# Turning the second half's x: TensorE transposes against 32x32 squares and VectorE transposes

## The chip, the cores and the metric

The kernel runs on one core of a Trainium2 chip. The time is device microseconds of one execution. A profile shows one execution in detail: the instructions of TensorE (PE for matmuls, PEld for weight loads), VectorE (DVE), ScalarE (ACT) and GpSimd (POOL), and the queue of SyncE (SP), which issues nearly all transfers between HBM and the on-chip memory SBUF. Matmul results land in PSUM, in banks of 128 partitions by 512 f32.

## The reference: gated experts and a residual

For x of 8 batches, 512 positions and 256 features, each of 8 experts and one shared expert computes a gated layer with 1024 hidden columns, and the results are added to x with weights per batch:

```
g = h @ Wg[e];  u = h @ Wu[e]                  # 256 -> 1024
expert[e] = (silu(g) * u) @ Wd[e]              # 1024 -> 256
mixed = sum_e gates[b, e] * expert[e]          # 8 experts
shared = (silu(h @ Sg) * (h @ Su)) @ Sd
out = x + (1 - s[b]) * mixed + s[b] * shared   # h is x
```

## The kernel before

**Algorithm and passes.** The batches are taken in two passes (`h` = 0 and 1) of `NI` = 4 batches each. In a pass the 4 batches are combined with 4 column groups of the weights by a scheme of sums and differences with the points `CI` = 0, 1, -1, 2, so that fewer products are needed. A unit is one pass, one expert and one half of the hidden columns: 2 x 9 x 2 = 36 units, run one after another. The first half of a unit's work is `gate_up` (P, Q, R1 and R steps, L404 to L469), the second is `down` (L501 to L606), which runs interleaved with the next unit's `gate_up`.

**How x gets its layout.** The matmuls contract over features, so x must lie with the features on the partitions: `[128 features, 2 halves, 512 positions]`. `load_rows` (L147) brings a batch in as rows, position `4p + t` on partition p. TensorE transposes against an identity matrix turn it, four 128x128 blocks into one PSUM bank (`turn`, L143), and ScalarE or VectorE copies the bank to SBUF. VectorE also forms x0 - c*x1 there, for the batches with c not zero.

For the first pass `turn_x` (L157) does this at the very start. For the second pass `prepare(1)` (L178) does it as background work. It is a Python generator, and the main loop takes one step of it (L836) at every fifth step of `down` from the third unit on. For each of the four batches it loads the rows into buffers of `iopool` (4 buffers of 128x512 f32), lets two steps pass, turns and copies half 1 (L191 to L196), then half 0, and stores both in `xd` in HBM (L200). Afterwards, for each of six pairs of batches, it loads `f` tiles back from `xd` (L208), lets GpSimd form sums and differences, and stores them in `xs`. The second pass loads `v` and `b` from there; the first pass has written its own `xs` from what the first unit forms with VectorE and GpSimd (L238, L240, L252, L253).

**PSUM banks of `down`.** `new_po` (L134) deals out two banks, po0 and po1. A turn takes the next bank without moving the counter (`turns=True`) and sets `turned`. `seeded` (L524) normally copies an accumulator into the bank with ScalarE (L530), lets the matmul add to it, and copies it back (L539); after a turn in that bank it does a plain matmul, and `put` (L505) adds the result to the accumulator on VectorE (L518).

**What sets the order.** `HAND` (L770) names TensorE and GpSimd: their instructions run in the order of the program text. ScalarE does so in the first unit alone. The order of VectorE, of ScalarE later on and of SP is chosen by a scheduler when the kernel is built: it places an instruction as soon as its inputs and buffers are there by its own estimate. On the chip each queue then runs strictly in that order.[...]

Of the kernel before, what the change touches and what calls it, by code (L numbers as in the profile page):

```python
# [11 lines left out]
ALU = mybir.AluOpType  # L12
# [4 lines left out]
def kernel(  # L17
# [37 lines left out]
    nc = tc.nc  # L55
    B, S, D = x.shape
    E, _, F = Wg.shape
    P = 128
    NT = S // P
    NE = E + 1  # L60
    NI = 4
    GRP = F // (NI * P)
    NH = B // NI
    CI = (0.0, 1.0, -1.0, 2.0)
# [22 lines left out]
    iopool = ctx.enter_context(tc.tile_pool(name="io", bufs=4))  # L87
# [10 lines left out]
    ve = nc.vector  # L98
# [31 lines left out]
    turned = [False, False]  # L130
# [3 lines left out]
    def new_po(name, turns=False):  # L134

        k = po_next[0]
        if held[k]:
            k = 1 - k
        if not turns:
            po_next[0] = 1 - k  # L140
        return ps_o.tile([P, S], F32, tag=f"po{k}", name=name), k

    def turn(bank, blocks):  # L143
        for t, block in enumerate(blocks):
            nc.tensor.transpose(bank[:, ts(t, P)], block, ident)

    def load_rows(pool, tag, b):  # L147
        rows = []
        for c in range(2):
            t = pool.tile([P, 2, D], F32, tag=tag, name=f"xin{b}_{c}")  # L150
            nc.sync.dma_start(
                t, x[b].rearrange("(p t) d -> p t d", t=NT)[:, 2 * c : 2 * c + 2, :]
            )
            rows.append(t)
        return rows

    def turn_x(h, rows):  # L157

        for i in range(NI):
            xt = xpool.tile([P, 2, S], F32, tag="x", name=f"x{h}_{i}")  # L160
            for n_, k in enumerate((0, 1) if CI[i] == 0.0 else (1, 0)):
                pt, n = new_po(f"ptx{h}_{i}_{k}")
                turn(pt, [rows[i][t // 2][:, t % 2, ts(k, P)] for t in range(NT)])
                turned[n] = True
                if k == 1:
                    nc.scalar.copy(xt[:, 1], pt)
                elif CI[i] == 0.0:
                    ve.tensor_copy(xt[:, 0], pt)  # L168
                else:
                    ve.scalar_tensor_tensor(  # L170
                        xt[:, 0], xt[:, 1], -CI[i], pt, ALU.mult, ALU.add
                    )
                if n_ == 1:
                    xhub[h, i] = xt
                yield

    def prepare(h):

        def tile_of(name):
            return iopool.tile([P, S], F32, tag="io", name=f"{name}{h}")  # L180

        for i in range(NI):
            to = xdram[h, i] = dram.tile([P, 2, S], F32, tag=f"xd{h}_{i}", name=f"xd{h}_{i}")
            rows = load_rows(iopool, "io", NI * h + i)
            yield
            yield
            both = {}
            for k in (1, 0):
                pt, n = new_po(f"ptx{h}_{i}_{k}", True)
                turned[n] = True  # L190
                turn(pt, [rows[t // 2][:, t % 2, ts(k, P)] for t in range(NT)])  # L191
                both[k] = tile_of(f"xt{i}_{k}_")
                if k == 1 or CI[i] == 0.0:
                    nc.scalar.copy(both[k], pt)
                else:
                    ve.scalar_tensor_tensor(both[0], both[1], -CI[i], pt, ALU.mult, ALU.add)  # L196
                yield
            yield
            for k in (1, 0):
                nc.sync.dma_start(to[:, k], both[k])  # L200
            yield
        for p, (i, j) in enumerate(PAIRS):
            d = CI[i] - CI[j]
            to = dram.tile([P, 3, S], F32, tag=f"xs{h}_{p}", name=f"xs{h}_{p}")
            at = []
            for n, k in ((i, 0), (j, 0), (j, 1), (i, 1)):
                t = tile_of(f"f{p}_{n}_{k}_")
                nc.sync.dma_start(t, xdram[h, n][:, k])  # L208
                at.append(t)
            yield  # L210
            yield
            v = at[0]
            gp.tensor_tensor(v, v, at[1], ALU.subtract)
            if d != 1.0:
                gp.tensor_scalar(v, v, 1.0 / d, 0.0, ALU.mult, ALU.add)
            yield
            gp.tensor_tensor(at[2], v, at[2], ALU.add)
            yield
            gp.tensor_tensor(at[3], v, at[3], ALU.add)
            yield  # L220
            yield
            yield
            for k, n in ((0, 0), (1, 2), (2, 3)):
                nc.sync.dma_start(to[:, k], at[n])
            scratch[h, p] = to
            yield
# [551 lines left out]
    for i in range(NI):  # L778
        loaded.append(load_rows(hpool, "h", i))
        load_w(units[0], i)  # L780
    turning = turn_x(0, loaded)
    for _ in range(2):
        next(turning)
# [4 lines left out]
    for i in range(NI):  # L788
        make_at(units[0], i)
    behind, acc, ahead = iter(()), {}, prepare(1)  # L790
    for u in units:
        final = u.closes
# [5 lines left out]
        for what in FIRST if u.n == 0 else LAST if nxt is None else ORDER:  # L798
# [27 lines left out]
            elif what == "X":  # L826
                i, j, pools = TAILS.pop(0)
# [59 lines left out]
```

## Time and profile before

| | |
|---|---|
| median of 3 runs | 2461.21 us (2460.86 to 2461.64) |
| the profiled execution | 2461.27 us |
| its span in the profile | 2459.3 us |
| turns of the second pass (L145, tile xin, 100 to 450 us) | 32 matmuls of 128x128, from 178.8 us on |
| ScalarE copies and VectorE forms after them (L194, L196) | 5 and 3, between 180 and 431 us |
| stores of xd (L200) | 8, between 180.5 and 431.1 us |
| VectorE busy, 20 to 40 us and 40 to 60 us | 19.93 and 17.69 of 20 us |
| GpSimd busy, 20 to 40 us and 40 to 60 us | 19.30 and 19.36 of 20 us |

The profile page first gives each engine's busy time, then the chain of work that ended last, followed back from the end. A timeline row gives start and length in microseconds, engine, line, operation, output and inputs; a bracket at the end gives the idle time before it and who ended it. Matmuls are pipelined and their ends modelled, so the distance of starts tells more than their lengths.

### The profile page before, as it was taken

To read this page: it belongs to the slowest core of one execution; us is meant where nothing else is said; L and a number is where in the kernel's file an instruction comes from. 1 tells how busy PE (TensorE), PEld (TensorE's weight loads), DVE (VectorE), ACT (ScalarE), POOL (GpSimd) and SP (SyncE) were. 2 spreads that over 40 slices of the span, in tenths; PEclk is the share of its full clock that TensorE was granted. 3 is DMA by queue.
4 is the path that set the end of the run, shared out by engine and by line. 5 is a ranking of instruction groups with operands and counts; after the bars stand their busy time and mean duration, and the time that the engine had idled before them with its cause. 6 is when DMAs were issued, how large, how long until landed. Compare 5 with 4: busy or idle time off the path is not lost.

```text
span 2459.3 us, 22816 instructions
## 1 busy us (share of the span) xinstructions
PE 2440.4 (99%) x5782; PEld 1084.0 (44%) x5782; DVE 1931.9 (79%) x2876; ACT 1246.4 (51%) x2305; POOL 2092.8 (85%) x2335
## 2 busy tenths in 40 slices
PE   9999999999999999999999999999999999999998
PEld 4444444444444444444444444444444444444444
DVE  7777787787777777777987777778777777777787
ACT  4555445545555555455455555555555555555543
POOL 7988888898898998888878888888888888888883
PEclk9999999999999999999999999999999999999999
DMA  5333333443333333333443233223333333223332
GB/s 168 95 93 103 97 113 107 124 132 107 109 115 94 119 97 106 110 116 113 127 144 94 88 90 98 86 86 99 99 103 103 94 103 90 86 89 96 91 93 82
DMA packets 180801, 255.83 MB, mean 104 GB/s; under 512 B 14016, under 2 KB 114368, under 8 KB 180672
## 3 DMA queue, kind: packets, MB, share of 16 engines
q1 hardware_dynamic: 180384, 254.33, 34.1%
q8 instruction: 49, 0.80, 0.1%
q14 instruction: 80, 0.66, 0.1%
q10 hardware_dynamic: 288, 0.04, 0.0%
HBM read 238.59 MB, written 15.73 MB: 103 GB/s over the span
## 4 chain that ended last, share of the span: by engine, by line
PE 89%; POOL 6%; DVE 2%; issue 1%; ACT 0%; DMA 0%; DVEq 0%; POOLq 0%; ACTq 0%
PE c L461 28%; PE c L451 14%; PE c L429 9%; PE c L407 9%; PE r L547 7%; PE r L570 7%; PE S L531 5%; PE b L531 5%; PE q L547 5%; PE s L547 2%; POOL cols L488 2%; POOL rows L488 1%; POOL wb L345 0%; DVE h L398 0%; POOL wb L346 0%
## 5 line engine op out<-in xcount | busy, mean ns | idle before, releaser
L461 PE MATMUL c<-b,wb 128*128 128x512 f32 x1728 | 847.3, 592 | 0.0
L393 ACT ACTIVATE sg<-c 128x512 f32<-128x512 f32 x576 | 343.6, 597 | 590.0 <-DVE c L466 336.9
L398 DVE SCALAR_TENSOR_TENSOR h<-sg,coef,c 128x512 f32<-128x512 f32 x576 | 428.1, 743 | 247.5 <-PE c L461 139.8
L461 PEld LDWEIGHTS c<-b,wb 128*128 128x128 f32 x1728 | 327.8, 190 | 410.0 <-issue 388.7
L451 PE MATMUL c<-v,u 128*128 128x512 f32 x864 | 441.7, 593 | 0.4 <-ACT c L446 0.3
L488 POOL TENSOR_TENSOR rows<-rows,h 128x512 f32<-128x512 f32 x282 | 371.1, 1316 | 0.0
L456 DVE TENSOR_TENSOR c<-D,c 128x512 f32<-128x512 f32 x432 | 299.1, 693 | 78.5 <-ACT sg L393 58.5
L488 POOL TENSOR_TENSOR cols<-cols,h 128x512 f32<-128x512 f32 x282 | 359.9, 1276 | 0.0
L466 DVE TENSOR_TENSOR c<-c,D 128x512 f32<-128x512 f32 x432 | 298.8, 692 | 20.1 <-PE c L461 19.9
L345 POOL TENSOR_TENSOR wb<-u,wb 128x256 f32<-128x256 f32 x108 | 79.0, 732 | 237.3 <-ACT wb L343 237.3
L407 PE MATMUL c<-x,w 128*128 128x512 f32 x576 | 277.9, 595 | 0.3 <-DVE x L168 0.3
L451 PEld LDWEIGHTS c<-v,u 128*128 128x128 f32 x864 | 162.9, 190 | 205.9 <-issue 165.3
L547 PE MATMUL r<-h,wd 128*128 128x512 f32 x426 | 217.7, 592 | 0.2 <-DVE xt L196 0.2
L570 PE MATMUL r<-X,ud 128*128 128x512 f32 x426 | 217.6, 592 | 0.0
L477 DVE TENSOR_TENSOR X<-h,h 128x512 f32<-128x512 f32 x213 | 210.4, 988 | 6.9
L429 PE MATMUL c<-x,at 128*128 128x512 f32 x432 | 209.6, 593 | 2.5 <-DVE P L422 2.2
L439 ACT COPY D<-c 128x512 f32<-128x512 f32 x284 | 165.9, 584 | 87.2 <-DVE h L398 87.2
L488 POOL TENSOR_TENSOR rows<-h,h 128x512 f32<-128x512 f32 x144 | 198.4, 1378 | 0.0
L488 POOL TENSOR_TENSOR cols<-h,h 128x512 f32<-128x512 f32 x144 | 184.2, 1279 | 0.0
L412 ACT COPY P<-c 128x512 f32<-128x512 f32 x216 | 126.6, 586 | 111.4 <-PE c L407 107.0
L407 PEld LDWEIGHTS c<-x,w 128*128 128x128 f32 x576 | 109.1, 191 | 135.0 <-issue 112.1
L530 ACT COPY S<-accS 128x512 f32<-128x512 f32 x134 | 79.1, 590 | 150.4 <-DVE accV L518 142.6
(105 smaller groups left out, 3482.4 us busy)
## 6 DMA issues: line engine op xcount, KB each, us to landing
b<-xs SPq DMA_DIRECT2D x210, 512.0 KB, 3.6
v<-xs SPq DMA_DIRECT2D x210, 256.0 KB, 2.6
w<-in_L_cond_Wg_dram SPq DMA_DIRECT2D x128, 128.0 KB, 3.5
w<-in_L_cond_Wu_dram SPq DMA_DIRECT2D x128, 128.0 KB, 3.6
wd<-in_L_cond_Wd_dram SPq DMA_DIRECT2D x32, 512.0 KB, 4.9
xin<-in_x_dram SPq DMA_DIRECT2D x24, 256.0 KB, 3.4
f<-xd SPq DMA_DIRECT2D x24, 256.0 KB, 3.2
xs<-f SPq DMA_DIRECT2D x18, 256.0 KB, 2.0
```

Of the source, the lines that this page charges most:

```text
L393: nc.scalar.activation(s, bank, AF.Silu)
L398: ve.scalar_tensor_tensor(t, u.sg[i, j], coef[:, u.e, b : b + 1], bank, ALU.mult, ALU.mult)
L407: nc.tensor.matmul(bank, u.raw[i][:, m, 0], xhub[u.h, i][:, 0], start=True, stop=True)
L429: nc.tensor.matmul(bank, u.at[i][:, m], xhub[u.h, i][:, 1], start=False, stop=True, skip_group_check=True,)
L451: nc.tensor.matmul(bank, u.U[p][:, m], u.V[p], start=False, stop=True, skip_group_check=True)
L456: ve.tensor_sub(other, u.Ds[j, m], bank)
L461: nc.tensor.matmul(bank, u.W[p][:, r, m], u.VB[p][:, r], start=False, stop=True, skip_group_check=True,)
L466: ve.tensor_add(bank, bank, u.Ds[j, m])
L488: gp.tensor_tensor(sums[n], u.h_[n, n] if first else sums[n], u.h_[at], ALU.add)
L531: nc.tensor.matmul(po, w, b, start=not full, stop=True, skip_group_check=full)
L547: nc.tensor.matmul(po, w, b, start=True, stop=True)
L570: nc.tensor.matmul(A, u.Ud[p], u.X[p], start=False, stop=True, skip_group_check=True)
```

## The change

In `prepare`, each half of a batch is loaded by four transfers (`load_turned`) instead of the whole batch by two. Transfer q brings 32 features of the half to partitions 32q to 32q+31. On the way the positions are arranged so that every 32x32 square of the tile holds 32 positions by 32 features, in pieces of 32 f32, 128 bytes. One VectorE transpose of 128x512 turns every square in place of the four TensorE transposes and writes SBUF directly. For half 0 of the batches with c not zero a VectorE instruction then forms xt0 - c*xt1 from SBUF. The column order of the result differs from before only in how it comes about: column t*128 + p still is position 4p + t. The first pass's `turn_x` stays as it was.

```diff
+    def load_turned(to, b, k):
+        at = x[b].rearrange("(c r t) d -> r t c d", r=32, t=NT)
+        for q in range(4):
+            nc.sync.dma_start(
+                to[ts(q, 32)].rearrange("r (t c d) -> r t c d", t=NT, d=32),
+                at[:, :, :, ts(4 * k + q, 32)],
+            )
+
@@ prepare
-            rows = load_rows(iopool, "io", NI * h + i)
+            rows = [tile_of(f"xin{i}_{k}_") for k in range(2)]
+            for k in (1, 0):
+                load_turned(rows[k], NI * h + i, k)
             yield
             yield
             both = {}
             for k in (1, 0):
-                pt, n = new_po(f"ptx{h}_{i}_{k}", True)
-                turned[n] = True
-                turn(pt, [rows[t // 2][:, t % 2, ts(k, P)] for t in range(NT)])
                 both[k] = tile_of(f"xt{i}_{k}_")
-                if k == 1 or CI[i] == 0.0:
-                    nc.scalar.copy(both[k], pt)
-                else:
-                    ve.scalar_tensor_tensor(both[0], both[1], -CI[i], pt, ALU.mult, ALU.add)
+                ve.transpose(both[k], rows[k])
+                if k == 0 and CI[i] != 0.0:
+                    ve.scalar_tensor_tensor(
+                        both[0], both[1], -CI[i], both[0], ALU.mult, ALU.add
+                    )
                 yield
```

## The prediction

> **What bounds the kernel now.** I read the page first: engine sums, then the chain that ended last.
>
> ```profile
> span 2459.3 us, 22816 instructions
> PE 2440.4 (99%) x5782; PEld 1084.0 (44%) x5782; DVE 1931.9 (79%) x2876; ACT 1246.4 (51%) x2305; POOL 2092.8 (85%) x2335
> PE 89%; POOL 6%; DVE 2%; issue 1%; ACT 0%; DMA 0%; DVEq 0%; POOLq 0%; ACTq 0%
> ```
>
> TensorE is the bound: 89% of the chain. So a TensorE instruction taken out is worth its pitch, and work given to VectorE costs nothing where VectorE has slack and its full length where the chain runs through VectorE. The next question is therefore where each side of the change lies. The removed turns, in TensorE's timeline (start, length, line; in brackets the idle time before and its releaser):
>
> ```profile
> 178.41 1.02 PE L570 MATMUL r<-X,ud 128*128 128x512 f32 x2
> 179.26 0.60 PE L145 MATMUL ptx<-ident,xin 128*128 128x128 f32 x4
> 179.70 1.02 PE L451 MATMUL c<-v,u 128*128 128x512 f32 x2
> ...
> 193.69 0.65 PE L145 MATMUL ptx<-ident,xin 128*128 128x128 f32 x4 [0.95 <-ACT accS L539]
> 194.18 1.88 PE L461 MATMUL c<-b,wb 128*128 128x512 f32 x4
> ```
>
> Ends are modelled and overlap, so pitches count: four turns take 0.44 us from start to start (179.26 to 179.70), a pair of 128x512 matmuls 0.86. The second group also waited 0.95 us for its PSUM bank, which ScalarE had still to copy out (L539). The waits add up over the whole run in
>
> ```profile
> PE ptx L145 <- ACT accS L539: 1.8, 2, 0.9
> ```
>
> Now the place where the new work goes. The order of the changed kernel's instructions shows that it does not stay at 180 to 430 us. TensorE's order, written by hand, had pinned the turns there; the new loads and transposes touch neither TensorE nor GpSimd, so the scheduler puts them where their inputs and buffers allow: all eight transposes stand in VectorE's queue between the rows that now start at 32 and at 105 us, in the first unit and a half. There VectorE (19.93 of 20 us busy between 20 and 40 us) looks like this:
>
> ```profile
> 31.57 0.82 DVE L240 TENSOR_SCALAR v<-v 128x512 f32<-128x512 f32 x1
> 32.32 0.69 DVE L456 TENSOR_TENSOR c<-D,c 128x512 f32<-128x512 f32 x1
> 32.92 0.69 DVE L466 TENSOR_TENSOR c<-c,D 128x512 f32<-128x512 f32 x1
> 33.52 0.94 DVE L238 TENSOR_TENSOR v<-x,x 128x512 f32<-128x512 f32 x1
> 34.38 0.73 DVE L398 SCALAR_TENSOR_TENSOR h<-sg,coef,c 128x512 f32<-128x512 f32 x1
> 35.15 0.70 DVE L456 TENSOR_TENSOR c<-D,c 128x512 f32<-128x512 f32 x1
> ...
> 37.54 0.73 DVE L398 SCALAR_TENSOR_TENSOR h<-sg,coef,c 128x512 f32<-128x512 f32 x1
> 38.30 1.67 DVE L477 TENSOR_TENSOR X<-h,h 128x512 f32<-128x512 f32 x1
> ```
>
> No row has idle time before it. And the chain, cut out for 36 to 40 us (start, length, what), runs through these rows:
>
> ```profile
> 37.61 0.67 DVE h L398
> 38.28 0.02 issue
> 38.30 0.60 ACT c L446
> 38.90 0.04 issue
> 38.95 1.14 PE c L451 x2
> ```
>
> **The change part by part.** *Removed from TensorE:* 8 groups of four turns, 8 x 0.44 = 3.5 us, all on the bound. The two bank waits, 1.75 us, go with them: the next user of that bank comes one or two pairs (0.86 us each) later, about the length of the wait. Together 5.2 us, bounds 3.5 and 5.4. The five ScalarE copies (L194, 0.59 each) and three VectorE forms (L196, 0.68) vanish at a time when both have gaps (they are hidden behind TensorE at full rate there), so nothing. Two accumulations that followed a turn (one of accS, one of accb) now go through the seeded path, a ScalarE copy in and one out, because `turned` is no longer set; 134 of those run already (L530), with 3 waits of TensorE at L531, 1.7 us in all, so two more are worth 0.03 us: nothing.
>
> *Added to VectorE:* 8 transposes of 128x512 f32. The trace has none. The nearest rows from below are one-source SBUF rows (L240, 0.41 us when GpSimd leaves the port free), from above two passes over the data, 1.4 us. I take the rate[...] that the 128x512 rows with 0.69 us have (L456, L466); one source spares it the collisions of the two-source SBUF rows (L477, 0.68 to 1.67). With the waits on four loads, 21 ns for each extra semaphore instruction (shortest at L398), 0.75 us each.
> The first (x of batch 4, half 1) stands behind L240 at 31.57, the second behind the h at 34.38. Queued behind both is the h at 37.54, whose end releases ScalarE's seeding copy at 38.30 and the matmul at 38.95, for which TensorE already waits 0.33 us. Nothing covers them: 2 x 0.75 = 1.5 us, bounds 0.8 and 2.8.
> The third stands before the h at 50.17, which now waits 0.85 us for TensorE: hidden. The fourth transpose falls behind the h at 61.6, and the three forms xt0 = xt1*(-c)+xt0, which now read two SBUF operands (about 1.2 us by L477's range instead of 0.68 from PSUM), at 66, 89 and 105 us. The fourth transpose and the first form meet gaps of 0.92 and 1.06 us, which take them. The fifth, sixth and seventh transpose meet gaps of 1.46, 1.01 and 1.65 us: hidden; without these gaps each would cost its 0.75. The form at 89 us stands before the six L422 rows, the first three of which free the bank of the matmul at 91.70: 89.33 + 3 x 0.61 = 91.16, plus 1.2 is 92.36, 0.66 us late. The eighth transpose and the last form at 105 us delay h by 1.6 us, of which ACT's seed has all but 0.3 in hand.
> These two-source forms also hold up GpSimd, which is the chain between 48 and 95 us: its 128x512 adds take 1.28 us alone and 1.73 beside such a form. Two forms before 96 us, 2 x 0.45 = 0.9 us, and TensorE waits at 95.90 for exactly that queue (0.6 us now). It runs beside the 0.66, so the larger counts: 0.9, bounds 0 and 1.4. Sum of the losses: 1.5 + 0.9 + 0.2 = 2.6 us.
>
> *Moved on SP's queue:* eight 256 KB loads become 32 of 64 KB, and they, the eight stores of xd and the first loads of f move from 180 to 440 us into 12 to 107. The first piece takes the old load's slot at 12.6, the next stands at 25.11; behind the store at 25.93 come two pieces, a store of v, and four pieces, then the v stores that wait for VectorE anyway. Issue: w loads with 256 rows take 0.43 and 0.47 us, wd with 512 takes 0.42, so 0.47: 6 x 0.47 + 0.4 = 3.2 us, the last issued at about 29.1. Landing: wd has 32 pieces for each of 16 engines as a square load has, and lands 4.9 us after issue, 1.5 of it for 32 pieces of 1 KB at 46 ns. The DMA records give 512 B 27 ns, 256 B 15 to 18, 32 B 7 to 9; so 128 B about 11 ns, 0.35 us for 32, landing 3.4 + 0.35 = 3.8 us, at 32.9. The second transpose is reached at 35.15 + 0.75 = 35.9: a margin of 3 us; the first has 1.7. Later stores of xd hold SP until their transposes are done, but v, b and w of the next unit have slack behind them (b issued at 67 is used at 97.7, v issued at 94.5 at 108).
>
> A rule of the Trainium skill speaks against this: "DMA: Bandwidth & Descriptors", specifications, wants at least 512 bytes per piece, below which the engine reads, modifies and writes. By the rows a 128 B piece costs 11 ns. By the rule I would cost it as two passes of a 512 B piece, an estimate of 54 ns, 1.7 us a load: the six from 26.4 land at 26.4 + 3.4 + 6 x 1.7 = 40.0, and VectorE would stand 4.1 us at the second transpose. The sum would be a loss of 1.5 us, 2462.7, instead of a gain of 2.6. The 256 and 32 B records show no such step (though they are few and read one row again and again), so I take the row and keep the 4.1 us for the range.
>
> *Sum:* against the profiled execution, 2461.3 us (2459.3 of span and 2.0 around it): -5.2 + 2.6 = -2.6, 2458.7. The median is 0.1 us below that execution: 2458.6 us.
>
> **The rivals.**
> *Squares late (slower).* No load of the trace has three steps on its DRAM side (rows, quarters of the batch, t). If each holds SP for c us instead of 0.47, seven pieces and about 1.1 us of stores between 25.1 and 31.9 (35.9 less about 4 of landing) allow 0.8 us each; beyond that VectorE stands 7 x (c - 0.8), and TensorE with it. From c = 1.2 the gain is gone; at 2 us the loss is 8.4 us: 2458.6 + 8.4 = 2467; at 3 us 2474. For it: the queue is in order and the two transposes follow closely. Against: issue time does not grow with the number of rows in any group.
> *Dear transposes.* At 1.4 us each the first two cost 2.8 and the later ones overrun their gaps by 0.4 to 0.6, about 1.5 in all: 2458.6 + 1.3 + 1.5 = 2461.4, no change.
> *No price.* If VectorE's rows, which run closely behind one another, hide the transposes after all (one that fills the port waits at L238 or L252, 0.2 to 0.9 us above their free length), only the gain of 5.2 counts: 2456.0.
>
> **How the numbers follow.** About 0.2%, 4.9 us, is what a measurement of this kernel can tell from no change, so the borders are 2456.3 and 2466.1. Small gain (2456.3 to 2460.5): 0.40. No price: 0.15, faster. Dear transposes or a small stall (2460.5 to 2466.1): 0.17. Squares late: 0.28, slower. That gives faster 0.15, same 0.57, slower 0.28. The range runs from 2455.5 (5.7 us less: the whole gain and the resolution of the waits) to 2473 (late squares at nearly 3 us); its two ends leave out 0.2. The likeliest case's own range is 2456.3 to 2460.5.
>
> **What would show it.** Right: no L145 between 180 and 430 us and 3.5 us less there; transposes of about 0.7 us in VectorE's timeline from 32 us on; the matmul now at 38.95 about 1.5 us later; no VectorE idle released by a DMA. The squares' row in the list of DMA issues gives issue and landing: 0.47 and 3.8 us. Wrong: issue above 0.8 us, a wait of the transposes on xin of more than 1 us, transposes over 1 us, or TensorE waits for ScalarE that reappear where the turns were.

## The result and the profile after

The changed kernel takes 2456.17 us (2455.52 to 2457.36, 17 runs), the kernel before beside it 2460.86 (2460.18 to 2461.64, 17 runs): a ratio of 0.9982, 95% interval 0.9975 to 0.9988. In a later group it took 2456.04 against 2461.03, 0.9980 (0.9971 to 0.9989). So the change gains 4.7 to 5.0 us, 0.2%, where 2.6 were forecast. The time lies inside the range on record, just under the lower end of the likeliest case's own.

The page of the changed kernel:

```profile
span 2454.0 us, 22789 instructions
...
PE 2434.6 (99%) x5750; PEld 1080.4 (44%) x5750; DVE 1936.1 (79%) x2882; ACT 1246.3 (51%) x2304; POOL 2094.7 (85%) x2335
...
PE 91%; POOL 6%; DVE 2%; issue 1%; DMA 0%; ACT 0%; SPq 0%; DVEq 0%; POOLq 0%; ACTq 0%
```

TensorE has 32 matmuls fewer and is still the bound. Its timeline where the first two groups of turns stood (start, length, line, operation):

```profile
178.82 1.02 PE L580 MATMUL r<-X,ud 128*128 128x512 f32 x2
179.68 1.02 PE L461 MATMUL c<-v,u 128*128 128x512 f32 x2
...
191.70 1.02 PE L541 MATMUL S<-h,wd 128*128 128x512 f32 x2
192.55 1.88 PE L471 MATMUL c<-b,wb 128*128 128x512 f32 x4
```

From pair to pair it is 0.86 us everywhere, with no wait at either place. The price is to be sought earlier. All of TensorE's waits between 30 and 110 us (in brackets, with who ended them):

```profile
34.75 1.13 PE L461 MATMUL c<-v,u 128*128 128x512 f32 x2 [0.43 <-ACT c L456]
39.02 1.12 PE L461 MATMUL c<-v,u 128*128 128x512 f32 x2 [0.57 <-ACT c L456]
92.08 1.12 PE L439 MATMUL c<-x,at 128*128 128x512 f32 x2 [0.72 <-DVE P L432]
96.32 1.12 PE L557 MATMUL q<-cols,ad 128*128 128x512 f32 x2 [0.54 <-POOL cols L498]
```

Before, the matmul at 38.95 waited 0.33 us and the one at 95.90 waited 0.60; the waits at 34.75 and 92.08 are new. VectorE's rows ahead of them:

```profile
31.56 0.70 DVE L202 STREAM_TRANSPOSE xt<-xin 128x512 f32<-128x512 f32 x1
...
35.10 0.70 DVE L202 STREAM_TRANSPOSE xt<-xin 128x512 f32<-128x512 f32 x1
...
36.90 0.79 DVE L262 TENSOR_TENSOR b<-v,x 128x512 f32<-128x512 f32 x1
37.61 0.73 DVE L408 SCALAR_TENSOR_TENSOR h<-sg,coef,c 128x512 f32<-128x512 f32 x1
38.38 0.98 DVE L487 TENSOR_TENSOR X<-h,h 128x512 f32<-128x512 f32 x1
...
88.64 1.59 DVE L204 SCALAR_TENSOR_TENSOR xt<-xt,xt 128x512 f32<-128x512 f32 x1
90.16 3.66 DVE L432 TENSOR_TENSOR P<-P,c 128x512 f32<-128x512 f32 x6
```

The transposes stand where they were forecast and take 0.70 us. But the b row after them takes 0.79 where it took 1.25, so that h starts at 37.61 against 37.54 before (X, behind it, takes 0.98 where it took 1.67). The rows ahead began 0.76 us earlier in this profile (29.11 against 29.87), so h is 0.8 us late by the two transposes, not 1.5. The groups of the new operations (duration in ns, smallest, median, largest):

```profile
L202 DVE STREAM_TRANSPOSE xt<-xin x8: 697/700/706, 31.6 to 104.2; 128x512 f32<-128x512 f32 x8
...
L204 DVE SCALAR_TENSOR_TENSOR xt<-xt,xt x3: 792/898/1590, 65.8 to 106.0; 128x512 f32<-128x512 f32 x3
...
L162 SPq DMA_DIRECT2D xin<-in_x_dram x32: 580/634/2162, 12.7 to 96.6; - x32
...
DMA to landing us min/median/max: 2.3/3.0/6.0
```

A square load holds SP for 0.63 us and lands 3.0 us after issue; no transpose of VectorE waits for one.

Single profiles are to be compared with care: at 26 us, up to where TensorE does the same in all of them, the profiles of these kernels differ by up to 2.5 us. The clock that TensorE is granted there makes part of it. The same window before and after (window and its length in us, busy time and instructions of PE, PEld, DVE, ACT and POOL, then the granted clock, the DMA share and GB/s):

```profile
8.00:11.40 3.40, 3.40 (x7) 1.45 (x6) 0.00 (x0) 0.89 (x2) 1.21 (x5) 0.50 1.08 352
```

```profile
8.00:11.40 3.40, 3.40 (x15) 1.93 (x14) 0.58 (x1) 1.66 (x3) 1.14 (x4) 1.00 0.99 314
```

At half the clock the profile of before falls 1.5 us behind by 12 us. So I set the starts of the 5750 common matmuls of two traces against each other and read only how the distance changes from one to the next. Between before and after the eight removed groups give back 0.40, 1.61, 0.44, 0.44, 1.57, 0.44, 0.44 and 0.43 us, and 0.37 comes from a wait of TensorE for a form, shown below: 6.1 us in all. The matmul at 92.08 loses 0.82 to 0.9.

### The profile page after: what moved, and what is told of

It is laid out like the page before. It is cut to its first block, busy times and chain, and to the rows that moved or that the text cites. A ratio compares the mean times of both kernels' runs of the same rounds, so it can differ in the third digit from the quotient of the medians.

```text
span 2454.0 us, 22789 instructions
## 1 busy us (share of the span) xinstructions
PE 2434.6 (99%) x5750; PEld 1080.4 (44%) x5750; DVE 1936.1 (79%) x2882; ACT 1246.3 (51%) x2304; POOL 2094.7 (85%) x2335
## 4 chain that ended last, share of the span: by engine, by line
PE 91%; POOL 6%; DVE 2%; issue 1%; DMA 0%; ACT 0%; SPq 0%; DVEq 0%; POOLq 0%; ACTq 0%
PE c L471 29%; PE c L461 14%; PE c L439 9%; PE c L417 9%; PE r L557 7%; PE r L580 7%; PE S L541 5%; PE b L541 5%; PE q L557 5%; PE s L557 2%; POOL cols L498 1%; POOL rows L498 1%; POOL wb L355 0%; DVE h L408 0%; POOL u L343 0%
```

## The experiments

They ran in three groups, each beside its own runs of the kernel before, at 2460.71, 2460.59 and 2461.03 us; I compare differences to these. The 95% intervals reach about 2.2 us to either side (0.09%), so by them alone only experiment 8 stands clear of the changed kernel. The single runs part more kernels: all 8 of experiment 1 (at most 2455.34) lie below all 22 of experiments 2 and 3 (at least 2455.80), and all 7 of experiment 11 (at most 2454.45) below all 11 of the changed kernel beside them (at least 2455.61). Where less than a microsecond divides two kernels, the reading rests on the aligned starts of one profile each.

**1. Without the turning.** The squares, transposes and forms are left out; the second pass works on unturned rows.

```diff
-                load_turned(rows[k], NI * h + i, k)
+                nc.sync.dma_start(
+                    rows[k].rearrange("p (t d) -> p t d", d=D),
+                    x[NI * h + i].rearrange("(p t) d -> p t d", t=NT)[:, 2 * k : 2 * k + 2, :],
+                )
...
-                both[k] = tile_of(f"xt{i}_{k}_")
-                ve.transpose(both[k], rows[k])
-                if k == 0 and CI[i] != 0.0:
...
+                both[k] = rows[k]
```

> The changed kernel without any turning for the second pass: whole rows loaded, no TensorE turns, no VectorE transposes, no xt0 - c*xt1; the second pass then works on x that was never turned, which alters its values and not its work. It measures the TensorE part alone. Theory of the prediction (losses of 2.6 us lie in the changed kernel): 2456.2 - 2.6 = 2453.6 us. Theory from the trace (the VectorE work costs TensorE 0.3 us at the first two transposes and 0.8 us at the form before 91 us, 1.1 in all): 2455.0 us. Rival, that the new VectorE work costs nothing: 2456.2 us, and the whole gain is the turns'.

Measured: 2455.08 us, 5.6 under before, ratio 0.9975 (0.9965 to 0.9985). That is the number of the second theory (2455.0), whose split is tested in experiment 4. The removal alone is worth 5.6 us, and all the new work on VectorE and SP costs 0.6 to 0.9, not 2.6. TensorE in this kernel:

```profile
46.41 1.12 PE L459 MATMUL c<-v,u 128*128 128x512 f32 x2 [1.51 <-ACT c L454]
```

and VectorE:

```profile
39.36 1.20 DVE L246 TENSOR_TENSOR v<-x,x 128x512 f32<-128x512 f32 x1 [1.23 <-POOL b L261]
...
43.39 1.69 DVE L260 TENSOR_TENSOR b<-v,x 128x512 f32<-128x512 f32 x1
45.00 0.73 DVE L406 SCALAR_TENSOR_TENSOR h<-sg,coef,c 128x512 f32<-128x512 f32 x1
```

Here the waits at 34.75 and 39.02 are missing, and TensorE is 2.1 us ahead of the changed kernel at 38 us (0.9 of it from the first 26 us, 1.2 from the two waits). It doesn't keep it: VectorE has to wait 1.23 us for GpSimd's b at 39.36, its own b takes 1.69 where it takes 1.01 in the changed kernel, and TensorE waits 1.51 us at 46.41, where the changed kernel doesn't wait. Behind that wait 0.4 of the 2.1 are left, and 0.1 at 50 us.

**2. Each transpose twice.**

```diff
                 ve.transpose(both[k], rows[k])
+                ve.transpose(both[k], rows[k])
```

> The changed kernel with every VectorE transpose done twice into the same tile: the same result, eight more VectorE instructions of 0.63 us pitch, most in the first 110 us. Theory (the first two transposes were nearly free only because shorter port waits of the two-source rows after them, b and X, made up for them, and nothing is left to make up for two more): 1.0 to 1.5 us slower than the changed kernel, about 2457.4 us. Rival (VectorE has room there after all): within 0.3 us of the changed kernel, 2456.2 us.

Measured: 2456.34 us, 0.9982 (0.9973 to 0.9991), 4.4 under before: 0.3 to 0.6 us more than the changed kernel for 5.6 us of VectorE work, and the theory of that moment (1.0 to 1.5) falls. Up to 91 us, with twelve transposes done instead of six, the aligned starts show no loss against the changed kernel. Behind that VectorE's order is another: no form stands ahead of the P rows, so their wait is gone (0.9 us), TensorE waits 0.5 us longer for GpSimd at 96.02, and a new wait at 113.31 costs 0.9. The few tenths are the sum of these shifts, and no price of a transpose can be read from them.

**3. The flag of the turned bank still set,** so that the two accumulations after a turn stay on the unseeded path.

```diff
                 both[k] = tile_of(f"xt{i}_{k}_")
+                n = po_next[0]
+                turned[1 - n if held[n] else n] = True
```

> The changed kernel with the flag of a turned bank still set as before, so that the same two accumulations go by a plain matmul and a VectorE add as in the kernel before, instead of by the seeded path. Theory of the prediction: worth nothing, 2456.2 us within 0.3. Rival: a part of the gain, up to 0.5 us for each of the two, belongs to the seeded path: 2456.7 to 2457.2 us.

Measured: 2456.36 us, 0.9981 (0.9972 to 0.9990). Also 4.4 under before. By the aligned starts this kernel and the changed one don't part at either accumulation (259.9 and 414.4 us): the two more seeded ones cost nothing. The few tenths more are a wait of TensorE for GpSimd's wb at 516.00 us, 0.5 us by the starts, that the changed kernel hasn't; what it has to do with the edit stays open.

**4. Without the forms.** The three instructions xt0 - c*xt1 are left out.

```diff
-                if k == 0 and CI[i] != 0.0:
-                    ve.scalar_tensor_tensor(
-                        both[0], both[1], -CI[i], both[0], ALU.mult, ALU.add
-                    )
```

> The changed kernel with the three forms xt0 - c*xt1 left out (half 0 of three batches of the second pass goes on unformed). Theory (the form at 88 us ahead of the six P rows is 0.8 of the 1.1 us): 2455.4 us, 2455.0 to 2455.8, no wait of TensorE for the P row at 92 us beyond the one before. Rival (the transposes at 32 and 36 us cost it all): 2456.2.

Measured: 2454.96 us, 5.6 under before, 0.9978 (0.9969 to 0.9987): the same gain as with nothing turned at all. By the aligned starts the kernel parts from the changed one at one place alone, the matmul at 92.08, by 0.9 us. So the eight transposes and the 32 loads cost nothing that the runs can tell, and what is paid is paid for the three forms. TensorE without them:

```profile
90.25 1.02 PE L457 MATMUL c<-v,u 128*128 128x512 f32 x2
91.10 1.02 PE L435 MATMUL c<-x,at 128*128 128x512 f32 x2
...
95.33 1.13 PE L553 MATMUL q<-cols,ad 128*128 128x512 f32 x2 [0.63 <-POOL cols L494]
```

The wait for the P row is gone. GpSimd beside the place of the first form, here and then in the changed kernel, where a form starts at 65.79:

```profile
65.90 1.26 POOL L494 TENSOR_TENSOR rows<-h,h 128x512 f32<-128x512 f32 x1
```

```profile
65.99 1.72 POOL L498 TENSOR_TENSOR rows<-h,h 128x512 f32<-128x512 f32 x1
...
89.62 0.92 POOL L383 TENSOR_TENSOR ud<-wd,ad 128x128 f32<-128x128 f32 x1
```

The add takes 0.46 us longer beside the form, and the ud at 89.62, which takes 0.46 elsewhere, another 0.46 beside the second: 0.9 us by which GpSimd's queue is late.

**5. One form taken away from the P rows.** The transpose ahead of the form at 88.64 is held back, by a copy of one column of the last h of the running unit, which VectorE has to take first. All background work behind it comes later too: three transposes and two forms go to 348 to 369 us, and only the first form stays in the first 110.

```diff
             u.h_[i, j] = t
+            mark[0] = t
...
+                if (i, k) == (2, 0):
+                    ve.tensor_copy(both[k][:, 0:1], mark[0][:, 0:1])
                 ve.transpose(both[k], rows[k])
```

> The changed kernel with one transpose alone held behind the last h at the step of the old turns, that of half 0 of the third batch; with it its form leaves the place ahead of the P rows at 88 us, while the first transposes stay at 32 and 36 us. A transpose (0.6 us) of the fourth batch then stands ahead of six other P rows, near 347 us, where 0.8 us fit. Theory (the form at 88 us is the price, the first two transposes cost little): 0.8 us less than the changed kernel, 5.5 under the kernel before, 2455.2 where that is at 2460.7. Rival (a VectorE row ahead of P rows costs its length): 0.2 less than the changed kernel, 2455.8.

Measured: 2456.08 us, 0.9981 (0.9972 to 0.9990), beside 2456.04 for the changed kernel in the same group: nothing gained. Its TensorE shows why:

```profile
97.18 1.12 PE L561 MATMUL q<-cols,ad 128*128 128x512 f32 x2 [1.12 <-POOL cols L502]
```

The P row's wait is gone, but the wait for GpSimd is 1.12 us, 0.49 more than without forms: the first form, at 67.06 us here, still stretches an add by 0.45, and what had run beside the P row's wait now stands alone. By the aligned starts 0.9 us are won at the P row and 0.6 lost at this wait; another 0.2 is lost at 361.89, beside six P rows that now have a transpose ahead of them. The expectation had left the price at GpSimd out.

**6. That form in two halves.**

```diff
-                    ve.scalar_tensor_tensor(
-                        both[0], both[1], -CI[i], both[0], ALU.mult, ALU.add
-                    )
+                    n = 2 if i == 2 else 1
+                    for _ in range(n):
+                        ve.scalar_tensor_tensor(
+                            both[0], both[1], -CI[i] / n, both[0], ALU.mult, ALU.add
+                        )
```

> The changed kernel with one of the three forms, that of the third batch ahead of the six P rows at 88 us, in two equal halves (xt0 - c/2*xt1, done twice; same result). Theory (the 0.8 us of room there is used up by the one form): TensorE waits the whole of the second as well, 0.65 us if GpSimd leaves the port free to 1.6 if not: 0.7 to 1.5 us more than the changed kernel, 2456.9 to 2457.7 where the kernel before is at 2460.7. Rival (VectorE has room there, and the wait seen in one profile is chance): within 0.3 us of the changed kernel.

Measured: 2456.29 us, 0.9981 (0.9972 to 0.9990), 0.25 more than the changed kernel. It doesn't test what it was made for: only one half stands ahead of the P rows, and the other was put behind them, at 107.12 us. TensorE waits 0.75 us at the P row, as with one. How the wait grows with more work ahead of the P rows stays unmeasured.

**7. Two groups of turns left out of the kernel before,** so that half 0 of the second pass's first and third batch goes on unturned.

```diff
             for k in (1, 0):
+                if k == 0 and i in (0, 2):
+                    both[k] = rows[k].rearrange("p t d -> p (t d)")
+                    yield
+                    continue
```

> The kernel before with two of the eight groups of turns left out, half 0 of the second pass's first and third batch (their rows go on unturned): the two whose first turn waited for a bank. Trace reading (these two are worth 1.6 us each, the others 0.4): 2460.8 - 3.2 = 2457.6 us, 2457.2 to 2458.1. The forecast's sizes (0.44 and the wait of 0.9 each, 1.3 a group): 2458.2. Rival (the wait only moves on to the next user of the bank, every group is worth its four turns): 2459.9.

Measured: 2458.57 us, 2.0 under before, 0.9991 (0.9983 to 1.0000). All three numbers miss, since I had the wrong group: the second wait for a bank belongs to half 1 of the third batch, and is still there,

```profile
335.69 0.66 PE L145 MATMUL ptx<-ident,xin 128*128 128x128 f32 x4 [0.81 <-ACT accS L543]
```

so one group with a wait and one without were taken out. The aligned starts say 1.61 + 0.44 = 2.05 us for these (1.60 and 0.44 in this kernel's own trace), and 2.0 was measured, with an interval of 0 to 4.2.

**8. Loads held back by GpSimd.** A one-column memset in GpSimd's order, which is written by hand, keeps the squares from being loaded before the old loads' place.

```diff
             for k in (1, 0):
+                gp.memset(rows[k][:, 0:1], 0.0)
                 load_turned(rows[k], NI * h + i, k)
```

> The changed kernel with its loads held back: GpSimd, whose order is written by hand, clears one column of each tile before its four loads, so loads, transposes and stores stay at 180 to 430 us, where the turns had been, and 32 GpSimd-ordered waits replace the free choice of the scheduler. Theory (the price is paid only because the transposes stand in the first 110 us, where VectorE has no gaps before what TensorE waits for): the 1.1 us come back, 2455.0 us, or 2453.6 if the price was the predicted 2.6. Rival (the price is that of VectorE work anywhere): 2456.2 us, no gain over the changed kernel. If loads of 128-byte pieces in the steady stream delay v, b or w: slower than 2456.2.

Measured: 2474.71 us, 1.0054 (1.0041 to 1.0067): 18.5 us slower than the changed kernel, where I expected 1.1 less. SP, VectorE and TensorE (each a timeline of this kernel):

```profile
161.23 5.52 SPq L162 DMA_DIRECT2D xin<-in_x_dram  x8
```

```profile
166.09 0.71 DVE L203 STREAM_TRANSPOSE xt<-xin 128x512 f32<-128x512 f32 x1 [9.44 <-POOL wd L389]
...
252.63 0.71 DVE L203 STREAM_TRANSPOSE xt<-xin 128x512 f32<-128x512 f32 x1 [8.84 <-DMA xin<-in_x_dram]
```

```profile
168.63 2.08 PE L440 MATMUL c<-x,at 128*128 128x512 f32 x2 [9.27 <-DVE P L433]
170.50 1.91 PE L542 MATMUL b<-rows,wd 128*128 128x512 f32 x2
172.20 1.91 PE L462 MATMUL c<-v,u 128*128 128x512 f32 x2
173.91 1.35 PE L440 MATMUL c<-x,at 128*128 128x512 f32 x2
175.10 1.02 PE L558 MATMUL q<-cols,ad 128*128 128x512 f32 x2
```

VectorE reached the transpose at 156.7 us. GpSimd came to the memset only at 161.11, so the loads were issued from 161.23 on, and VectorE, whose order is fixed, stood with everything behind it. The profile names a GpSimd instruction on another tile as releaser of the first wait; the loads are issued from 161.23 on, 0.69 us each, so the fourth at 163.3, and with 2.7 us of landing (median of these eight) it is there at 166.0, where the transpose starts. Two of the eight transposes did so; by the aligned starts they cost TensorE 12.5 and 7.3 us.

**9. Loads and transposes both held, with a lead.** The same lateness of the loads, but by the mark on VectorE, and the transposes held as well, two steps of the background work later.

```diff
             for k in (1, 0):
+                ve.tensor_copy(rows[k][:, 0:1], mark[0][:, 0:1])
                 load_turned(rows[k], NI * h + i, k)
...
+                ve.tensor_copy(both[k][:, 0:1], mark[0][:, 0:1])
                 ve.transpose(both[k], rows[k])
```

> As the version that holds the transposes behind the last h, and the loads too: each half's four loads follow a one-column copy of the last h at the step of the old loads, two steps (some 15 us) ahead of their transposes. Theory (the 18.5 us of the version with loads held by GpSimd came from loads issued after VectorE had already reached the transposes that wait for them): with the lead no stall, 2455.1 us, 2454.7 to 2455.8. Rival (64 KB loads of 128-byte pieces in that stretch are themselves slow or hold up SP's queue for v, b and w of the next unit): at least 5 us slower than with early loads, 2460 or more.

Measured: 2456.42 us, 4.2 under before, 0.9982 (0.9974 to 0.9991). The 18.5 us are gone with no transpose earlier than 182.87 us: it was the order, loads after the transposes had been reached, and neither the late place nor the squares. It is 0.6 above the upper end of what I expected, and 1.2 above the next kernel, for a reason shown there.

**10. Transposes held, loads early.** As 9 without the mark on the loads.

> The changed kernel, but each transpose follows, in VectorE's order, a one-column copy of the last h of the running unit, so transposes and forms stand between about 165 and 430 us while the squares are still loaded early. Theory (the price of 1.1 us lies in the place: the form ahead of the P rows at 88 us and the beginning beside a full GpSimd): 2455.1 us, 2454.7 to 2455.6, no VectorE idle time released by a DMA or GpSimd at a transpose. Rival (VectorE's added work costs the same wherever it stands): 2456.2. Rival (the late place itself is what made the version with loads held by GpSimd 18.5 us slower): about 2474.

Measured: 2455.22 us, 5.4 under before, 0.9977 (0.9968 to 0.9986), as the theory had it. One new wait is left in the stretch. TensorE and VectorE there:

```profile
428.11 1.13 PE L442 MATMUL c<-x,at 128*128 128x512 f32 x2 [0.59 <-DVE P L435]
```

```profile
424.97 0.69 DVE L435 TENSOR_TENSOR P<-P,c 128x512 f32<-128x512 f32 x1
425.58 0.70 DVE L204 STREAM_TRANSPOSE xt<-xin 128x512 f32<-128x512 f32 x1
426.20 0.65 DVE L435 TENSOR_TENSOR P<-P,c 128x512 f32<-128x512 f32 x1
426.78 0.67 DVE L206 SCALAR_TENSOR_TENSOR xt<-xt,xt 128x512 f32<-128x512 f32 x1
427.37 2.47 DVE L435 TENSOR_TENSOR P<-P,c 128x512 f32<-128x512 f32 x4
```

The last transpose and form stand among the first three of the six P rows that free a bank. In experiment 9 the form at this place takes 1.60 us instead of 0.67, and the same matmul waits 1.52: 0.9 of the 1.2 us between the two.

**11. The last one past the P rows.** As 10, with one step more ahead of the last half.

```diff
             for k in (1, 0):
+                if (i, k) == (3, 0):
+                    yield
                 both[k] = tile_of(f"xt{i}_{k}_")
```

> As the version with the transposes held behind the last h, but the last transpose and form come one step of the background work later, behind the six P rows of their unit and not among them. Theory (about 0.8 us of VectorE work fits ahead of or among the first three of the six P rows; what is more, TensorE waits for, 0.59 us at 428 us in the version before): 0.6 us less than that version, 6.0 us under the kernel before, 2454.7 where that is at 2460.7, and no wait of TensorE for a P row in the stretch of the transposes. Rival (the difference of 0.9 us between the changed kernel and the held one has nothing to do with P rows): as the held version, 2455.3.

Measured: 2453.67 us (2452.99 to 2454.45), 7.4 under before, 0.9969 (0.9958 to 0.9981): faster than both kernels, by 2.4 us against the changed one in the same group. No wait is left between 160 and 480 us. That is 1.4 more than expected, and 2.0 more than experiment 10 (7.4 against 5.4); part of it lies far behind the change. The waits of TensorE for GpSimd's sums (total, times, longest) in the kernel of experiment 10 and in this one:

```profile
PE q L560 <- POOL cols L501: 3.2, 4, 1.2
```

```profile
PE q L562 <- POOL cols L503: 1.6, 3, 0.7
```

The rest of the background work, GpSimd's sums of f, follows one step later too, and two waits of 0.93 and 1.17 us near 840 and 1040 us, which the kernel before has as well, became none and one of 0.42; a new wait of 0.56 for a transfer of b stands at 850.97. By the aligned starts these are worth 0.7 us in the end, and the P rows 0.8. The remaining 0.5 of the 2.0 us stays open.

## Why the forecast was right, and where its sizes were off

The direction and the range held, and the main gain had the right cause. The range was wide, and most of it lay on the side of a loss. A gain of 0.18% in the first group and 0.20% in the last lies at the border that the forecast had drawn between no change (0.57) and faster (0.15). The size was 2.6 us and came out at 4.7 to 5.0. Term by term:

| step of the sum | forecast, us | measured, us | from |
|---|---|---|---|
| 8 x 4 turns | 3.5 gained | 3.5 | aligned starts, 0.44 a group |
| two bank waits | 1.75 gained | 2.3 | aligned starts, 1.61 and 1.57 less 0.44 each |
| vanished VectorE forms | 0 | 0.4 gained | aligned starts |
| together | 5.2 gained | 5.6 by runs, 6.1 by the trace | experiments 1 and 4 |
| first two transposes | 1.5 lost | 0 by runs, 0.2 by the trace | 4 against 1; aligned starts |
| GpSimd stretched, P row beside it | 0.9 lost | 0.6 to 0.9 | changed kernel against 4 |
| last transpose and form | 0.2 lost | none seen | changed kernel's waits |

*The step that failed: "Nothing covers them: 2 x 0.75 = 1.5".* The two transposes do delay TensorE, as the waits at 34.75 and 39.02 show. But the sum carried this delay to the end of the kernel. Seven kernels have these two transposes (the changed one and its repeat, experiments 2 to 6). Against the kernel before all seven fall back by 0.7 to 0.85 us between 30 and 42 us, and all but 0.15 to 0.27 of it is made up at 50. The six without them move by anything from 1.1 gained to 1.1 lost in this stretch. Up to 46 us VectorE, ScalarE and GpSimd release each other in a ring (b, h, the seeding copy, wb, b again), and two of them are nearly full: between 20 and 40 us of the changed kernel VectorE is busy 19.94 and GpSimd 18.79 of 20 us (ScalarE 8.31). A VectorE that comes earlier waits for GpSimd, and its two-source rows take longer (experiment 1: 1.23 us of waiting, b 1.69 instead of 1.01). That the transposes cost next to nothing in the end is shown by experiment 4 against 1 and by these seven traces; that the ring is the reason is read from the traces alone. The prediction had named both facts, GpSimd full there and on the chain from 48 us, and VectorE rows stretched by the port, the latter in its rival "No price" at 0.15. That rival's 2456.0 came within 0.2 us of the time, but by luck: the forms did cost what the likeliest case said, and the gain that both had put too small made up for it.

*Mis-sized: the waits removed.* A bracket counts from the modelled end of the matmul before, which lies 0.16 us behind the next start when nothing waits (length 1.02, pitch 0.86). So a wait delays by its bracket plus 0.16. This makes 0.3 of the 0.5 us missing from the two bank waits. And "nothing" for the vanished forms overlooked one of the kernel before:

```profile
273.17 1.02 PE L461 MATMUL c<-b,wb 128*128 128x512 f32 x2
274.40 1.12 PE L547 MATMUL r<-h,wd 128*128 128x512 f32 x2 [0.21 <-DVE xt L196]
```

1.23 us from start to start, 0.37 above the pitch: TensorE waited for the form to read its bank. Trace and runs differ by 0.5 us on the gain as a whole, which stays open.

*Right: GpSimd's 0.9 beside the P row's 0.66, "so the larger counts".* The two stretched instructions lose 0.45 us each, as put (the second was taken for a 128x512 add and is a ud of 128x128); the P row came at 0.72 (0.82 in the starts). Experiment 5 shows that they do run beside each other: with the P row's wait gone, the wait for GpSimd grows by 0.6. The Trainium skill's "GPSIMD Engine Reference" says in its opening table that GpSimd shares its SBUF interfaces with VectorE, and contends with VectorE instructions that have two SBUF inputs; 1.72 against 1.26 us agrees.

*Right: the seeded path is worth nothing* (experiment 3; the 134 named there are those of S, and 135 of b run beside them), and right were the transposes of 0.7 us in the queue between the rows at 32 and 105 us.

*The squares.* Issue takes 0.63 us, not 0.47, still below the 0.8 at which the rival "Squares late" begins; landing takes 3.0, not 3.8. The rule of 512 bytes, costed in the prediction at 54 ns a piece and a stall of 4.1 us, isn't borne out as a price: a piece of 128 bytes takes 13 ns (median of the 16384 in the trace; 512 bytes take 27), the square loads land as soon as the 256 KB row loads of the first pass (3.3 us), and no transpose waits for them. But experiment 8 shows that the mechanism of that rival is real: a transpose whose loads come late holds up everything, 18.5 us for two of them. What decides is when the load is issued, not how long it takes.

## What to carry over

A wait that new work causes early is only lost if no later wait takes it up: follow it through the next ring of engines before carrying it to the end of the sum, and count a removed wait by the distance of starts less the pitch, not by its bracket. Work that is free in itself is paid for by what stands behind it on its engine (here the P rows) and by what shares its port (GpSimd's adds), and the two don't add when they run side by side, so removing one of them alone gains little or, as here, nothing. Where one engine's order is fixed by estimate and another's by hand, hold a transfer and its user together, on the engine that uses it: a mark that is held by another engine, even a little late, costs a stall of everything behind.

## What the runs showed that I had not expected

After the stand of 9.27 us in experiment 8 TensorE doesn't start at full speed. The windows of that kernel (window and its length in us, busy time and instructions of each engine, then the granted clock, the DMA share and GB/s):

```profile
160.00:168.00 8.00, 0.00 (x0) 0.00 (x0) 1.91 (x4) 0.00 (x0) 7.69 (x12) 0.77 0.39 61
168.00:172.00 4.00, 3.37 (x4) 1.51 (x5) 3.58 (x6) 1.07 (x2) 0.12 (x1) 0.50 0.23 75
172.00:176.00 4.00, 4.00 (x8) 1.62 (x7) 1.33 (x2) 1.69 (x3) 0.73 (x1) 0.68 0.17 52
176.00:180.00 4.00, 4.00 (x11) 1.85 (x10) 2.53 (x5) 2.95 (x5) 0.00 (x0) 1.00 0.21 79
```

The granted clock is 0.50 in the window after the stand, and 1.00 only in the one from 176 us on (in finer windows, from 174.6 us). In the timeline shown with experiment 8 the pairs stand 1.7 to 1.9 us apart at first instead of 0.86, which costs about 3 us on top of the wait: four pairs from 168.63 to 175.10 take 6.47 us instead of 3.44. The Trainium skill's "TensorE: Matmul & The Clock Gate" (Part 1) states half the clock after an idle window of about 3.4 us, and full clock again after a busy one of that length, where the windows run on freely. The first whole window from 168.63 on would then end between 172.0 and 175.5 us, and 174.6 agrees. The second stand does not quite: TensorE's last matmul ahead of it ends at 250.8, and the granted clock falls at 253.1, after 2.3 us of idling; it is full again at 259.9. In the changed kernel, whose longest wait is 1.8 us, the granted clock is 1.00 from 10 us to 2440 us.

A two-source VectorE row of 128x512 f32 from SBUF takes anything between 0.68 and 1.70 us beside GpSimd's adds (b, X and the forms of the changed kernel). A transpose of the same size stays at 0.70 (0.687 to 0.712 over the 16 of experiment 2). Two transposes in front of h, 1.3 us from start to start, moved it by 0.8, because the b row behind them came out 0.46 us shorter.
